# A new order for the table that drives a Mamba layer: spreads, decays, gates and one convolved pair

## The chip, the core and the metric

The kernel runs on one core of a Trainium2 chip. The metric is the device time of one execution, in microseconds (us). A core has five engines that run side by side, each in its own program order, and that wait for each other through semaphores: TensorE (PE in the profile; its weight loads are PEld), VectorE (DVE), ScalarE (ACT), GpSimd (POOL), and SyncE (SP), which here only issues DMA transfers. Below, "SP's queue" is that list of transfers: it is issued in order, and a transfer that has to wait for something holds all that stand behind it.

## What is computed

The input is 4 batches of 256 tokens of 512 channels, all in float32. There are two layers. Layer 0 is a normalisation, an attention with latent queries and keys, and a gated feed-forward network (it is the same before and after the change). Layer 1 adds two branches to x: a Mamba mixer and a feed-forward network in which a router picks two of eight low-rank experts for each token. Cut to what matters here:

```python
xn = layernorm(x)
xz = xn @ in_proj_w                         # 512 -> 2 * 1024, split in x and z
xc = silu(conv_b + causal_conv4(x))         # 4 taps, each of 1024 channels on its own
dt_r, Bm, Cm = rmsnorm of (xc @ x_proj_w)   # 32, 16 and 16 columns
dt = softplus(dt_r @ dt_proj_w + dt_bias)   # (b, 1024, 256)
for t in range(256):                        # 1024 channels x 16 states
    h = exp(dt[t] * A) * h + dt[t] * Bm[t] * xc[t]
    y[t] = sum over the 16 states of h * Cm[t]
out = x + ((y + D * xc) * silu(z)) @ out_proj_w + moe_lora(xn)
```

## The kernel before

Layer 0 ends, and layer 1's scan begins, near 327 us of the profiled execution. Layer 1's scan is cut into 128 steps u = 32 b + 4 c + g: b is the batch (0 to 3), c one of 8 blocks of 128 channels, g one of 4 groups of 4 states. In a step, 128 partitions hold 32 channels by 4 states, and the 4 x 256 free elements are the block's four parts of 32 channels by the tokens. What a step needs:

- decays u (L1087 to L1102): four Exp on ScalarE (L1099) write exp(dt * A) into one of four rotating tiles, free once scan u-4 has read its tile. The first ten steps use borrowed tiles, whose first column GpSimd clears first (L1096).
- scan_in u (L1104): an instruction of VectorE that collects the step's waits, then bx = B * (dt * x) into PSUM (L1112). It waits for decays u, for hmul u-4 and sum u-4 (below), because h has four buffers, and at g = 0 for the spread of du.
- scan u (L1116): one scan instruction over time on VectorE (L1127).
- hmul u (L1132): h * C on GpSimd. sum u (L1139, L1150): four products on TensorE that add the states up into ysum, with D * xc ahead at g = 0 (L1148).
- After the four groups of a block: take (L1156, a ScalarE copy of ysum into xc) and gate (L1161, GpSimd: xc * silu(z)).

What feeds the steps, batch by batch, is cut into small actions:

- spread n b c (L1047): four DMAs of SP's queue that bring one block's dt or du (= dt * x) from device memory, 32 channels to all 128 partitions, into one of two buffers. dt and du get to memory through step_out (GpSimd, L1020, L1022, L1024, then a send on SP's queue, L1045) and step_x (GpSimd, L1037, then a send) for a pair of blocks.
- load_x, load_z: 512 KB of projection weights for a pair of blocks on SP's queue (L625), into one of three buffers. load_late: the weights of the router and of the output (L1463). store_x: 256 KB of x to the output (L1289), to which add_to (GpSimd, L1301) adds the branches later.
- px_mm and pz_mm (L792, L1064): the projections, on TensorE. conv_in (L798 to L831): ScalarE copies px into a padded tile and makes diagonal matrices of the taps. conv_taps (L833): four products with these matrices on TensorE for the first block of a pair (L847); for its second block either four more (if the pair is listed in `both`), or ScalarE scales the four shifted rows and GpSimd adds three of them up (L854). conv_out adds the bias, conv_silu takes the whole batch's silu.
- pp_mm, pp_square, pp_norm, step_in, step_exp: B, C and dt of a batch (L958 to L985: per block two ScalarE activations at L963 and L964, then four whole ones from L982). gate_silu: silu of z with a load of the activation table ahead and one behind (L1075).
- router, choose (15 small VectorE instructions from L1198 to L1230, one a call), expert_mid, expert_turn, dense, out_mm: the second branch and the output.

Nothing schedules this: the order of each engine is the order in which the program text issues it. The text is the table `plan`, with an entry for each step u, in up to four parts divided by "|". `play(u, 0)` runs the first part before bx u, `play(u, 1)` the second between bx u and scan u, the third and fourth after scan u and hmul u:

```python
    for u in range(total + 2):
        play(u, 0)
        if u < total:
            if u:
                scan_in(u)
            play(u, 1)
            scan(u, 1 if u < total - 1 else 4)
        ...
        play(u, 2)
        play(u, 3)
```

So "decays 12" in the first part of step 9 puts four Exp at that place of ScalarE's program, and "spread dt 0 3" four transfers at that place of SP's. "rest i" are the last pieces of layer 0's feed-forward network (two products of TensorE into po each, L470), "add_last" adds them to x on VectorE (L482), "open" frees layer 0's memory. Small PSUM tiles (px, pz, pt, pdt, pp, po) share three buffers.

Of the kernel before, what the change touches and what calls it, by code (L numbers as in the profile page):

```python
# [41 lines left out]
def block_kernel(  # L42
# [614 lines left out]
    def mark(*k):  # L657
        done.add(k)
# [137 lines left out]
    both = ((1, 0), (1, 3), (2, 2), (3, 1), (3, 3),)  # L796
# [614 lines left out]
    dt = dts[0, 0]  # L1411
# [47 lines left out]
    def load_late(n, k=0, of=1):  # L1459
# [4 lines left out]
        if k == of - 1:  # L1464
# [11 lines left out]
            "decays 5, one_out 3, norm_root 1 |  | decays 4, send_dt, step_x 0 1, "  # L1476
            "add_last 5 | sum 1, rest 23, rest 24, rest 25, rest 26, rest 27, rest 28, rest 29"
        ),
        3: "spread dt 0 2 | norm_stats 2 |  | sum 2, rest 30, rest 31, rest 32, rest 33, rest 34, rest 35",
        4: "norm_scale 1 |  | add_last 6, add_last 7 | sum 3, open",  # L1480
        5: (
            "take 0 0, decays 6, decays 8, pz_mm 0 0 0, norm_turn 1 0, decays 7, norm_turn 1 1, "
            "spread du 0 2, load_z 0 1 |  | norm_copy 1 0, norm_copy 1 1 | sum 4"
        ),
        6: "decays 9, load_x 1 0, pz_mm 0 0 1, step_in 0 1 0, step_in 0 1 1, load_x 1 1 |  |  | sum 5",
        7: (
            "px_mm 1 0 0, store_x 2, load_x 1 3, gate_silu 0 0, decays 10, "
            "spread dt 0 3 |  | store_x 3, gate 0 0 | sum 6"
        ),
        8: "px_mm 1 0 1, pz_mm 0 1 0, pz_mm 0 1 1, store_x 0, store_x 1, step_exp 0 1 |  |  | sum 7",  # L1490
        9: (
            "decays 12, take 0 1, load_late rl, step_out 0 1 0 0, conv_in 1 0, px_mm 1 1 0, "
            "load_x 1 2, spread du 0 3 |  |  | sum 8"
        ),
        10: "step_out 0 1 0 1, decays 11, store_x 4, store_x 5, decays 13, conv_taps 1 0, px_mm 1 1 1",
        11: (
            "decays 14, load_z 0 2, step_out 0 1 0 2, step_x 0 2, conv_in 1 1, spread dt 0 4, "
            "px_mm 1 2 0 |  | gate 0 1 | sum 9, sum 10"
        ),
        12: "decays 15, gate_silu 0 1, conv_taps 1 1, px_mm 1 2 1 |  |  | sum 11",  # L1500
        13: "take 0 2, decays 16, step_out 0 1 1 0, spread du 0 4, conv_in 1 2, px_mm 1 3 0 |  |  | sum 12",
        14: "decays 17, conv_taps 1 2, px_mm 1 3 1",
        15: "decays 18, step_out 0 1 1 1, conv_in 1 3, spread dt 0 5 |  | load_late lb | sum 13, sum 14",
        16: (
            "decays 19, step_out 0 1 1 2, load_late bw 1 4, conv_taps 1 3, "
            "spread du 0 5 |  |  | sum 15, pz_mm 0 2 0, load_late ow 0 8"
        ),
        17: (
            "step_x 0 3, take 0 3, conv_out 1 3, decays 20, load_z 0 3, pz_mm 0 2 1, "
            "conv_silu 1 0 2 |  | gate 0 3 | sum 16, gate 0 2"  # L1510
        ),
        18: "decays 21, load_late bw 0 4 |  |  | sum 17",
        19: "decays 22, pp_mm 1 0, spread dt 0 6 |  |  | sum 18",
        20: "decays 23, load_late ow 1 8, pp_mm 1 1, spread du 0 6 |  | load_late bw 2 4 | sum 19",
        21: "take 0 4, decays 24, load_late bw 3 4, pp_square 1, load_late ow 2 8 |  | gate 0 4 | sum 20",
        22: "decays 25, pz_mm 0 3 0, load_late ow 3 8 |  | pp_norm 1, step_in 1 0 0 | sum 21",
        23: (
            "decays 26, step_exp 1 0 0, step_in 1 0 1, load_z 1 0, c_send 1, load_late ow 5 8, "
            "step_exp 1 0 1 |  | spread dt 0 7 | sum 22"
        ),  # L1520
        24: "decays 27, load_z 1 1, router 0 0, pz_mm 0 3 1, load_late ow 6 8 |  |  | sum 23",
        25: (
            "take 0 5, load_late ow 4 8, decays 28, spread du 0 7, router 0 1, gate_silu 0 3, "
            "step_out 1 0 0 0, router 0 2 |  |  | sum 24"
        ),
# [24 lines left out]
        35: "decays 38, norm_turn 2 0, dense 0 1 1 | choose | choose, add_to 0 | sum 34",  # L1550
# [289 lines left out]
```

## Time and profile before

| | us |
|---|---|
| median of 3 runs | 833.2 (830.65 to 836.03) |
| the profiled execution, its own time | 832.04 |
| its span in the trace | 829.9 |
| bx 1 starts | 330.54 |
| bx 127 starts | 817.85 |

How to read the profile: the page lists the busy time of each engine and its share of the span, then groups of instructions by line and engine ("out<-in" by the program's names), with their count, busy time, mean duration of one, idle time of the engine just before them and what ended most of it. The trace can also be asked for the waits of an engine, and for a timeline of a stretch, where a number in brackets is the idle time ahead of an instruction and what ended it. "x4" merges like instructions that follow each other. The table of stages, from the trace:

```profile
326.88:380.91 54.03, 48.44 (x238) 32.55 (x237) 41.94 (x30) 42.32 (x96) 37.60 (x31) 0.94 0.57 159
380.91:446.20 65.29, 52.41 (x302) 34.57 (x301) 60.10 (x35) 58.46 (x132) 53.21 (x34) 0.90 0.67 175
446.20:498.40 52.20, 43.84 (x226) 23.29 (x228) 51.77 (x42) 44.07 (x100) 45.10 (x27) 0.84 0.46 123
498.40:654.60 156.20, 134.29 (x734) 78.67 (x726) 153.11 (x93) 132.00 (x307) 146.69 (x94) 0.94 0.57 143
654.60:744.10 89.50, 78.18 (x394) 38.49 (x395) 86.30 (x64) 67.83 (x149) 79.29 (x49) 0.89 0.45 112
744.10:817.85 73.75, 60.13 (x286) 25.57 (x285) 66.86 (x40) 43.22 (x96) 56.68 (x33) 0.95 0.42 91
```

The columns are the stretch (start and end, us), its length, the busy time (and number of instructions) of PE, PEld, DVE, ACT and POOL, the clock that TensorE was granted, the share of the DMA engines that was busy, and GB/s. The stretches run from bx to bx: 0 to 11, 11 to 28, 28 to 41, 41 to 84, then to just before 108, and to 127.

### The profile page before, as it was taken

To read this page: it belongs to the slowest core of one execution; us is meant where nothing else is said; L and a number is where in the kernel's file an instruction comes from. 1 tells how busy PE (TensorE), PEld (TensorE's weight loads), DVE (VectorE), ACT (ScalarE), POOL (GpSimd) and SP (SyncE) were. 2 spreads that over 40 slices of the span, in tenths; PEclk is the share of its full clock that TensorE was granted. 3 is DMA by queue.
4 is the path that set the end of the run, shared out by engine and by line. 5 is a ranking of instruction groups with operands and counts; after the bars stand their busy time and mean duration, and the time that the engine had idled before them with its cause. 6 is when DMAs were issued, how large, how long until landed. Compare 5 with 4: busy or idle time off the path is not lost.

```text
span 829.9 us, 11205 instructions
## 1 busy us (share of the span) xinstructions
PE 733.8 (88%) x3802; PEld 427.4 (52%) x3802; DVE 653.5 (79%) x589; ACT 553.2 (67%) x1126; POOL 511.5 (62%) x413
## 2 busy tenths in 40 slices
PE   4999999999999999988887879797997779897984
PEld 2665545666555676666544446443465445333431
DVE  4486756287644535896899999999999899988996
ACT  4335564434556367689978887889898797826760
POOL 3133232001333432767889889979799889896875
PEclk9799999999999999999998789799899889999997
DMA  7233332001222332266595527644756453364620
GB/s 228 64 102 95 110 93 72 1 1 39 77 77 77 119 58 64 80 178 200 116 287 139 159 59 184 151 128 102 178 130 163 89 128 103 101 142 125 115 50 26
DMA packets 72194, 91.48 MB, mean 110 GB/s; under 512 B 12653, under 2 KB 54185, under 8 KB 72010
## 3 DMA queue, kind: packets, MB, share of 16 engines
q1 hardware_dynamic: 60618, 67.44, 30.6%
q0 software_dynamic: 10800, 21.50, 10.8%
q10 hardware_dynamic: 720, 1.84, 0.7%
q8 instruction: 30, 0.49, 0.2%
q14 instruction: 26, 0.21, 0.1%
HBM read 68.15 MB, written 13.42 MB: 98 GB/s over the span
## 4 chain that ended last, share of the span: by engine, by line
PE 46%; ACT 17%; DVE 17%; POOL 8%; DMA 5%; issue 5%; SPq 1%; POOLq 0%; ACTq 0%; DVEq 0%
DVE h L1127 7%; ACT decay L1099 7%; PE pg L445 6%; PE pu L445 5%; POOL h L1132 5%; DVE bx L1112 5%; PE av L398 4%; PE po L470 3%; DMA dts<-dtd 3%; PE po L1276 3%; PE px L792 3%; PE scT L387 2%; DVE mpl L355 2%; PE ysum L1150 2%; PE px L847 2%
## 5 line engine op out<-in xcount | busy, mean ns | idle before, releaser
L1132 POOL TENSOR_TENSOR h<-h,cr 128x1024 f32<-128x1024 f32 (+1 forms) x129 | 301.8, 2352 | 60.1 <-DVE h L1127 47.4
L1127 DVE TENSOR_TENSOR_SCAN h<-decay,bx 128x1024 f32<-128x1024 f32 (+1 forms) x125 | 279.0, 2234 | 4.2
L1099 ACT ACTIVATE decay<-dts,aneg 128x255 f32<-128x255 f32 x492 | 205.7, 500 | 38.6 <-DMA dts<-dtd 16.1
L1112 DVE TENSOR_TENSOR bx<-brow,dus 128x1024 f32<-128x1024 f32 x128 | 157.6, 1231 | 23.7 <-ACT decay L1099 12.8
L1150 PE MATMUL ysum<-h,stack 128*32 128x256 f32 x1016 | 85.7, 417 | 28.8 <-POOL h L1132 28.8
L457 POOL TENSOR_TENSOR hlo<-g,hhi 128x512 fp32r<-128x512 f32 x28 | 35.9, 1280 | 114.6 <-ACT hhi L456 114.6
L355 DVE TENSOR_REDUCE mpl<-sc 128x4 f32<-128x1024 f32 x64 | 76.7, 1219 | 22.7 <-PE sc L353 21.2
L428 POOL DMA_DIRECT2D wgu<-in_wgu x56 | 31.0, 555 | 95.4 <-PE pg L445 94.3
L389 ACT ACTIVATE pe<-scT 128x1024 f32<-128x1024 f32 x64 | 64.0, 1023 | 22.9 <-PE sc L353 14.3
L1325 PE MATMUL po<-ow,xc 128*128 128x512 f32 x128 | 66.5, 640 | 0.4 <-DVE xc L1733 0.4
L1150 PEld LDWEIGHTS ysum<-h,stack 128*32 128x32 f32 x1016 | 21.9, 112 | 86.1 <-POOL h L1132 49.8
L792 PE MATMUL px<-xn1T,w_in 128*128 128x256 f32 x256 | 63.2, 398 | 1.5 <-ACT dt L964 1.0
L1064 PE MATMUL pz<-xn1T,w_in 128*128 128x256 f32 x256 | 62.8, 393 | 0.0
L792 PEld LDWEIGHTS px<-xn1T,w_in 128*128 128x128 f32 x256 | 49.8, 198 | 13.9 <-issue 2.4
L1064 PEld LDWEIGHTS pz<-xn1T,w_in 128*128 128x128 f32 x256 | 48.1, 194 | 16.2 <-issue 8.9
L453 DVE SCALAR_TENSOR_TENSOR g<-g,pg 128x512 f32<-128x512 f32 x28 | 19.2, 687 | 43.0 <-ACT g L452 43.0
L445 PE MATMUL pg<-xhi,wgu 128*128 128x512 f32 x112 | 49.7, 443 | 1.2 <-ACT xhi L245 1.2
L470 PE MATMUL po<-wd,hhi 128*128 128x512 f32 x112 | 49.8, 444 | 0.0
L445 PE MATMUL pu<-xhi,wgu 128*128 128x512 f32 x112 | 47.6, 425 | 0.8 <-DVE g L455 0.8
L456 ACT CAST hhi<-g 128x512 fp32r<-128x512 f32 x28 | 17.3, 620 | 45.8 <-DVE g L455 45.8
L445 PE MATMUL pg<-xlo,wgu 128*128 128x512 f32 x112 | 44.9, 401 | 0.7 <-DVE xlo L252 0.7
L445 PE MATMUL pu<-xlo,wgu 128*128 128x512 f32 x112 | 44.3, 396 | 0.0
(243 smaller groups left out, 1306.4 us busy)
## 6 DMA issues: line engine op xcount, KB each, us to landing
dts<-dtd SPq DMA_DIRECT2D x124, 128.0 KB, 3.5
dus<-dud SPq DMA_DIRECT2D x124, 128.0 KB, 3.4
wgu<-in_wgu POOLq DMA_DIRECT2D x56, 256.0 KB, 2.7
w_in<-in_inz SPq DMA_DIRECT2D x16, 512.0 KB, 5.5
w_in<-in_inx SPq DMA_DIRECT2D x14, 512.0 KB, 5.4
dtd<-dt SPq DMA_DIRECT2D x15, 256.0 KB, 2.1
dud<-du SPq DMA_DIRECT2D x15, 256.0 KB, 2.4
wd<-in_wd POOLq DMA_DIRECT2D x7, 512.0 KB, 3.7
```

The source lines that it names most:

```text
L355: nc.vector.tensor_reduce(mpl2[b % 2][:, qb, 2 * hp : 2 * hp + 2, 16 + 2 * gq : 18 + 2 * gq], sc.rearrange("p i (f k) -> p i f k", f=2), A ...
L389: nc.scalar.activation(pes[b, k][:, 2 * t : 2 * t + 2, :], sc, AF.Exp)
L445: mm(ps, lhsT=wgus[i][:, hc, :], rhs=xs[j][:, hc, :], start=(hc == 0 and j == 0), stop=(hc == HC - 1 and j == 1))
L470: mm(po, lhsT=hids[th][j][:, m, i * P : (i + 1) * P], rhs=wd[:, m, :], start=False, stop=(m == MC - 1 and j == 1))
L792: mm(px[:, i, :], lhsT=w[:, i, hc, :], rhs=xns[b][:, hc, :], start=(hc == 0), stop=(hc == HC - 1))
L1064: mm(pz[:, i, :], lhsT=w[:, i, hc, :], rhs=xns[b][:, hc, :], start=(hc == 0), stop=(hc == HC - 1))
L1099: made["da", u] = nc.scalar.activation(da[:, k, 1:], live["dts", b, c][:, k, 1:], AF.Exp, scale=aneg[:, c, k, g : g + 1])
L1112: nc.vector.tensor_tensor(bx, brow[g // 2][:, g % 2, :].unsqueeze(1).to_broadcast([P, NG, S]), live["dus", b, c], ALU.mult)
L1127: nc.vector.tensor_tensor_scan(h[:, n].rearrange("p n t -> p (n t)"), da[:, n].rearrange("p n t -> p (n t)"), bx[:, n].rearrange("p n t -> ...
L1132: made["hc", u] = (nc.vector if k == NG - 1 else nc.gpsimd).tensor_tensor(h[:, n], h[:, n], crows[b][:, g, :].unsqueeze(1).to_broadcast([P ...
L1150: made["sum", u] = mm(ysum[k * NB : (k + 1) * NB, :], lhsT=stack, rhs=hc[:, k, :], start=False, stop=(g == NU - 1))
L1325: mm(live["po", b, i], lhsT=xcs[b][:, c, i * P : (i + 1) * P], rhs=late_w["ow"][:, c, :], start=first, stop=last)
```

## The change

The diff has three parts. In `both` the pair (3, 3) is dropped: the second block of the last pair of batch 3 is convolved by ScalarE and GpSimd instead of TensorE. In the last step a line `need("sums", total - 1)` is added, which only states what must have been issued and issues nothing. All the rest is the table: the same actions (each issued once, as before) in another order, in nearly every step from 2 to 127. Spreads are issued in front of stores and late weights; decays, step_out, gates and products of TensorE stand elsewhere. Cut to the steps that the prediction speaks of most (the others are changed in the same manner):

```diff
-    both = ((1, 0), (1, 3), (2, 2), (3, 1), (3, 3),)
+    both = ((1, 0), (1, 3), (2, 2), (3, 1),)
...
-2: (
-    "decays 5, one_out 3, norm_root 1 |  | decays 4, send_dt, step_x 0 1, "
-    "add_last 5 | sum 1, rest 23, rest 24, rest 25, rest 26, rest 27, rest 28, rest 29"
-),
-3: "spread dt 0 2 | norm_stats 2 |  | sum 2, rest 30, rest 31, rest 32, rest 33, rest 34, rest 35",
-4: "norm_scale 1 |  | add_last 6, add_last 7 | sum 3, open",
-5: (
-    "take 0 0, decays 6, decays 8, pz_mm 0 0 0, norm_turn 1 0, decays 7, norm_turn 1 1, "
-    "spread du 0 2, load_z 0 1 |  | norm_copy 1 0, norm_copy 1 1 | sum 4"
-),
-6: "decays 9, load_x 1 0, pz_mm 0 0 1, step_in 0 1 0, step_in 0 1 1, load_x 1 1 |  |  | sum 5",
-7: (
-    "px_mm 1 0 0, store_x 2, load_x 1 3, gate_silu 0 0, decays 10, "
-    "spread dt 0 3 |  | store_x 3, gate 0 0 | sum 6"
-),
-8: "px_mm 1 0 1, pz_mm 0 1 0, pz_mm 0 1 1, store_x 0, store_x 1, step_exp 0 1 |  |  | sum 7",
-9: (
-    "decays 12, take 0 1, load_late rl, step_out 0 1 0 0, conv_in 1 0, px_mm 1 1 0, "
-    "load_x 1 2, spread du 0 3 |  |  | sum 8"
-),
-10: "step_out 0 1 0 1, decays 11, store_x 4, store_x 5, decays 13, conv_taps 1 0, px_mm 1 1 1",
-11: (
-    "decays 14, load_z 0 2, step_out 0 1 0 2, step_x 0 2, conv_in 1 1, spread dt 0 4, "
-    "px_mm 1 2 0 |  | gate 0 1 | sum 9, sum 10"
-),
-12: "decays 15, gate_silu 0 1, conv_taps 1 1, px_mm 1 2 1 |  |  | sum 11",
+2: (
+    "decays 5, one_out 3, norm_root 1 |  | send_dt, step_x 0 1, add_last 5 | sum 1, rest 23, "
+    "decays 4, rest 24, rest 25, rest 26, rest 27, rest 28, rest 29, rest 30, rest 31, "
+    "rest 32, rest 33, rest 34, rest 35"
+),
+3: "spread dt 0 2 | norm_stats 2",
+4: "norm_scale 1 |  | add_last 6, add_last 7 | sum 2, sum 3, open",
+5: (
+    "take 0 0, decays 6, pz_mm 0 0 0, norm_turn 1 0, norm_turn 1 1, spread du 0 2, "
+    "load_z 0 1 |  | norm_copy 1 0, norm_copy 1 1 | sum 4"
+),
+6: (
+    "decays 9, load_x 1 0, decays 8, decays 7, spread dt 0 3, pz_mm 0 0 1, store_x 1, "
+    "step_in 0 1 0, step_in 0 1 1, load_x 1 1, gate_silu 0 0 |  |  | sum 5"
+),
+7: "px_mm 1 0 0, load_x 1 3, decays 10 |  | gate 0 0 | sum 6",
+8: "px_mm 1 0 1, pz_mm 0 1 0, pz_mm 0 1 1, step_exp 0 1 |  |  | sum 7",
+9: (
+    "decays 12, take 0 1, px_mm 1 1 0, step_out 0 1 0 0, store_x 5, conv_in 1 0, "
+    "load_late rl, store_x 2, load_x 1 2 |  | gate 0 1 | sum 8"
+),
+10: (
+    "step_out 0 1 0 1, decays 11, store_x 4, decays 13, conv_taps 1 0, px_mm 1 1 1, "
+    "step_out 0 1 1 0 |  | spread du 0 3, step_out 0 1 1 1 | store_x 3"
+),
+11: (
+    "decays 14, load_z 0 2, step_out 0 1 0 2, step_x 0 2, conv_in 1 1, spread dt 0 4, "
+    "px_mm 1 2 0, gate_silu 0 1 |  |  | sum 9, sum 10"
+),
+12: "decays 15, conv_taps 1 1 |  |  | sum 11",
...
-13: "take 0 2, decays 16, step_out 0 1 1 0, spread du 0 4, conv_in 1 2, px_mm 1 3 0 |  |  | sum 12",
-14: "decays 17, conv_taps 1 2, px_mm 1 3 1",
-15: "decays 18, step_out 0 1 1 1, conv_in 1 3, spread dt 0 5 |  | load_late lb | sum 13, sum 14",
-16: (
-    "decays 19, step_out 0 1 1 2, load_late bw 1 4, conv_taps 1 3, "
-    "spread du 0 5 |  |  | sum 15, pz_mm 0 2 0, load_late ow 0 8"
-),
-17: (
-    "step_x 0 3, take 0 3, conv_out 1 3, decays 20, load_z 0 3, pz_mm 0 2 1, "
-    "conv_silu 1 0 2 |  | gate 0 3 | sum 16, gate 0 2"
-),
+13: "take 0 2, px_mm 1 2 1, spread du 0 4, conv_in 1 2, px_mm 1 3 0, step_out 0 1 1 2 |  |  | sum 12",
+14: "decays 16, conv_taps 1 2, decays 17, store_x 0, px_mm 1 3 1, conv_in 1 3",
+15: "decays 18, spread dt 0 5 |  | load_late lb | spread du 0 5, sum 13, sum 14",
+16: "decays 19, conv_taps 1 3 |  | decays 20 | pz_mm 0 2 0, sum 15",
+17: (
+    "step_x 0 3, take 0 3, conv_out 1 3, pz_mm 0 2 1, load_z 0 3, conv_silu 1 0 2, "
+    "load_late bw 1 4 |  |  | sum 16, load_late ow 0 8"
+),
...
-22: "decays 25, pz_mm 0 3 0, load_late ow 3 8 |  | pp_norm 1, step_in 1 0 0 | sum 21",
-23: (
-    "decays 26, step_exp 1 0 0, step_in 1 0 1, load_z 1 0, c_send 1, load_late ow 5 8, "
-    "step_exp 1 0 1 |  | spread dt 0 7 | sum 22"
-),
-24: "decays 27, load_z 1 1, router 0 0, pz_mm 0 3 1, load_late ow 6 8 |  |  | sum 23",
+22: (
+    "decays 25, spread du 0 6, load_z 1 0, load_late ow 1 8 |  | pp_norm 1, step_in 1 0 0, "
+    "gate 0 4 | sum 21"
+),
+23: (
+    "decays 26, step_exp 1 0 0, pz_mm 0 3 0, step_in 1 0 1, c_send 1, step_exp 1 0 1, "
+    "load_late bw 3 4, load_late ow 2 8 |  |  | sum 22"
+),
+24: (
+    "pz_mm 0 3 1, decays 27, router 0 0, load_late ow 3 8, "
+    "load_late ow 5 8 |  | spread dt 0 7 | sum 23"
+),
...
-31: "spread dt 1 1 | choose | choose, decays 34 | sum 30",
-32: (
-    "decays 35, spread du 1 1, step_out 1 0 1 2, b_rows 1 1, gate_silu 1 0 1, norm_root 2, "
-    "load_x 2 0 | choose | choose | sum 31"
-),
-33: (
-    "take 0 7, decays 36, gate 0 7, step_x 1 1, step_in 1 1 0, "
-    "dense 0 0 0 | choose | choose | sum 32"
-),
+31: "spread dt 1 1, pz_mm 1 1 1 |  | choose, decays 34",
+32: (
+    "spread du 1 1, step_out 1 0 1 2, sum 30, load_x 2 1, norm_root 2, load_x 2 0, "
+    "gate_silu 1 0 1, step_x 1 1 | choose, choose | b_rows 1 1, decays 35, choose | sum 31"
+),
+33: "take 0 7, dense 0 0 0, decays 36, step_in 1 1 0 | choose | choose | sum 32",
...
-36: (
-    "decays 39, spread du 1 2, step_out 1 1 0 0, norm_copy 2 0, norm_turn 2 1, "
-    "load_x 2 2 | choose | choose | sum 35"
-),
+36: (
+    "decays 39, step_out 1 1 0 0, norm_copy 2 0, norm_turn 2 1, "
+    "step_out 1 1 1 0 | choose | choose | sum 35"
+),
...
-41: "take 1 1, step_out 1 1 1 0, conv_taps 2 0, px_mm 2 1 1, px_mm 2 2 0 |  |  | sum 40",
-42: "decays 45, spread dt 1 4, decays 44, conv_in 2 1, px_mm 2 3 0 |  | gate 1 1 | sum 41",
+41: "take 1 1, conv_taps 2 0, px_mm 2 1 1, px_mm 2 2 1 |  |  | sum 40",
+42: "decays 45, load_z 1 3, conv_in 2 1, decays 44, px_mm 2 3 0 |  |  | sum 41",
...
-75: "px_mm 3 3 0, decays 78 |  | gate 2 1 | sum 74",
-76: "decays 79, spread du 2 4, load_z 2 3, conv_in 3 2, step_out 2 1 1 2 |  |  | sum 75",
-77: "take 2 2, step_x 2 3, decays 80, conv_taps 3 2, px_mm 3 3 1 |  |  | sum 76",
+75: "decays 78, step_out 2 1 1 0, step_out 2 1 1 1, step_out 2 1 1 2, conv_taps 3 1 |  |  | sum 74",
+76: "decays 79, spread du 2 4, load_z 2 3, px_mm 3 2 1, conv_in 3 2, px_mm 3 3 0 |  |  | sum 75",
+77: "take 2 2, gate 2 1, decays 80, conv_taps 3 2 |  |  | sum 76",
...
-80: "spread du 2 5, decays 83, pz_mm 2 2 1, conv_taps 3 3, conv_out 3 3 |  | gate 2 2 | sum 79",
+80: "decays 83, pz_mm 2 2 1, spread du 2 5, conv_taps 3 3, conv_out 3 3 |  |  | sum 79",
...
-104: (
-    "decays 107, out_mm 1 1 4, out_mm 1 1 5, out_mm 1 1 6, step_out 3 1 1 0, step_x 3 2, "
-    "spread du 3 3, load_z 3 2, spread dt 3 3 |  |  | sum 103"
-),
-105: "take 3 1, decays 108, out_mm 1 1 7 |  | gate 3 1, expert_mid 2 0 | sum 104",
-106: (
-    "decays 109, spread dt 3 4, out_mm 2 0 0, out_mm 2 0 1, step_out 3 1 1 1, "
-    "load_z 3 3 |  |  | sum 105"
-),
-107: "decays 110, step_out 3 1 1 2, out_mm 2 0 2, out_mm 2 0 3, out_mm 2 0 4, expert_turn 2",
+104: (
+    "decays 107, out_mm 1 1 4, out_mm 1 1 5, out_mm 1 1 6, step_out 3 1 1 0, spread du 3 3, "
+    "load_z 3 2, step_out 3 1 1 1, spread dt 3 3, out_mm 1 1 7 |  | expert_mid 2 0, "
+    "spread dt 3 4 | sum 103"
+),
+105: "take 3 1, decays 108, out_mm 2 0 0 |  |  | sum 104",
+106: "step_x 3 2, decays 109, out_mm 2 0 1, load_z 3 3 |  |  | sum 105",
+107: "out_mm 2 0 2, out_mm 2 0 3 |  |  | step_out 3 1 1 2",
...
+            need("sums", total - 1)
```

## The prediction

> **What bounds the kernel now.** I read the page first (busy shares, groups), then the starts of the VectorE instructions from 326 us on, then the table of VectorE's waits for that stretch, and last the timelines of ScalarE and of SP's queue around the longest two.
>
> ```profile
> PE 733.8 (88%) x3802; PEld 427.4 (52%) x3802; DVE 653.5 (79%) x589; ACT 553.2 (67%) x1126; POOL 511.5 (62%) x413
> ...
> L1132 POOL TENSOR_TENSOR h<-h,cr 128x1024 f32<-128x1024 f32 (+1 forms) x129 | 301.8, 2352 | 60.1 <-DVE h L1127 47.4
> L1127 DVE TENSOR_TENSOR_SCAN h<-decay,bx 128x1024 f32<-128x1024 f32 (+1 forms) x125 | 279.0, 2234 | 4.2
> L1099 ACT ACTIVATE decay<-dts,aneg 128x255 f32<-128x255 f32 x492 | 205.7, 500 | 38.6 <-DMA dts<-dtd 16.1
> L1112 DVE TENSOR_TENSOR bx<-brow,dus 128x1024 f32<-128x1024 f32 x128 | 157.6, 1231 | 23.7 <-ACT decay L1099 12.8
> ```
>
> TensorE has the highest share, but that is an average over two layers. Layer 1 is the 128 steps from bx 0 (326.88) to bx 127 (817.85), and in most of them VectorE runs without a hole: a bx (1.23 us), a scan (2.29) and two gaps of 0.035, 3.587 us a step. At that rhythm 127 steps would take 455.5 us; they took 491.0. The 35 us between are waits, VectorE's own other instructions and slow first steps:
>
> ```profile
> DVE bx L1112 <- ACT decay L1099: 12.8, 2, 8.3
> DVE bx L1112 <- PE ysum L1150: 5.5, 4, 2.1
> DVE x L482 <- PE po L470: 2.2, 1, 2.2
> ```
>
> (Columns: us in total, times, the longest.) A new order removes no step, so all it can win is in these lines and in VectorE's small instructions. By place, from the starts of bx: bx 11 waits 8.33 us, bx 17 1.83, bx 20 0.61, bx 27 1.37, bx 28 0.40, bx 85 2.14, bx 108 4.49, bx 110 1.11: 20.3 us. The two longest:
>
> ```profile
> 374.41 1.70 ACT L1099 ACTIVATE decay<-dts,aneg 128x255 f32<-128x255 f32 x4 [2.80 <-DMA dts<-dtd]
> 376.02 0.35 ACT L1156 COPY xc<-ysum 128x256 f32<-128x256 f32 x1
> 376.27 0.58 ACT L810 COPY pad<-px 128x512 f32<-128x512 f32 x1
> 376.75 1.28 ACT L815 ACTIVATE dg<-cst,vec 128x128 f32<-128x128 f32 x4
> 377.93 1.27 ACT L820 ACTIVATE tap<-cst,vec 128x128 f32<-128x128 f32 x4
> 379.10 3.29 ACT L1099 ACTIVATE decay<-dts,aneg 128x255 f32<-128x255 f32 x8
> ```
> ```profile
> 746.79 1.70 ACT L1099 ACTIVATE decay<-dts,aneg 128x255 f32<-128x255 f32 x4 [8.29 <-DMA dts<-dtd]
> ```
> ```profile
> 731.37 0.38 SPq L1045 DMA_DIRECT2D dtd<-dt  x1
> 736.13 0.38 SPq L1045 DMA_DIRECT2D dud<-du  x1
> 736.62 1.83 SPq L1053 DMA_DIRECT2D dus<-dud  x4
> 738.89 0.36 SPq L625 DMA_DIRECT2D w_in<-in_inz  x1
> 739.34 2.75 SPq L1053 DMA_DIRECT2D dts<-dtd  x6
> ```
>
> bx 11 comes after decays 11 (first half of the last row of the first fence, to 380.80), which stand behind conv_in 1 0, a take and decays 12; only the 2.80 us ahead of decays 12 are a transfer. bx 108 is a transfer alone: SP stood from 731.8 to 736.1 for du of pair 2 (step_x 3 2 on GpSimd), and the spread of dt 3 3 queued behind it.
>
> **The change part by part.** Each term is against the profiled execution, 832.04 us with a span of 829.9.
>
> Steps 2 to 11. (a) The rests of layer 0 run together with no sum between: one sum of 0.64 us less ahead of add_last 7, for which VectorE waited 2.2 us (L482); 0.65 earlier. (b) Decays 9 now stand in front of 8 and 7. They need GpSimd's memset (L1096), behind hmul 5, which ended at 356.79, now about 356.15. Decays 9, 8, 7 at 1.70 each end at 361.2, while scan 7 started at 359.38: about 1.9 us lost. (c) ScalarE is then busy without a hole: step_in (8 rows from 359.28 to 362.27, 2.9) to 364.1, gate_silu (3.2, from 362.29 to 365.5) to 367.3, decays 10 and step_exp (365.50 to 371.62, 6.1) to 373.4, decays 12 (1.7) to 375.1. No transfer is waited for: spread dt 0 3, issued at 367.26 behind load_x 1 3, now goes before it. take, conv_in and decays 11 as before, 374.41+1.61 to 380.80, 4.8: 379.9. So bx 11 starts near 380.0, **0.9 won**; (a) and (b) vanish in what is left of its wait, and 6 of its 8 us stay, because ScalarE's queue is full where before it stood for a DMA.
>
> bx 17 waited for sum 13, on TensorE behind a conv_taps (3.55 us) and a px_mm (1.89). The taps of pair 3 and its px now come after or a step earlier, the sum ends between 399.9 and 401.7 and bx 17 is due at 401.6: **1.6 won** of 1.83 (bounds 0 and 1.83). bx 20: send dt and its spread go earlier, **0.6**. bx 21: decays 21 follow conv_silu in step 17 and no decays 20 stand between: **0.4 lost**. bx 27 and 28: step_in 1 0 1 waited behind pz on TensorE; pz_mm 0 3 0 is now behind step_exp, and decays 27 end about 437.6 where bx 27 is due about 438.5: **1.8 won** (1.37+0.40).
>
> choose, steps 30 to 39, are VectorE instructions:
>
> ```profile
> L1221 DVE TENSOR_TENSOR sel<-sel,b 128x32 f32<-128x32 f32 x1 | 1.4, 1394 | 0.0
> ...
> L1206 DVE TENSOR_TENSOR sel<-sel,m 128x32 f32<-128x32 f32 x1 | 0.2, 195 | 0.0
> ```
>
> The same operation takes 0.2 or 1.4 us: those between a bx and its scan end when GpSimd's hmul ends, those just behind a scan find GpSimd between two instructions. Four two-input ones stood in front of a scan (L1200, L1209, L1217, L1221), four do so after (L1202, L1209, L1217, L1221). GpSimd has more behind it there (step_x 1 1 a step earlier, step_out 1 1 1 0 four): **0.5 lost**, bounds 1.2 won (one such less) and 5.9 lost (below). The Trainium skill, GPSIMD Engine Reference, section Key points, says that GpSimd shares its SBUF interfaces with VectorE and contends with instructions of two SBUF inputs; the rows agree (1.4 us against 0.2). By that rule alone each two-input choose is at risk, wherever GpSimd is late.
>
> Step 42: decays 44 behind conv_in 2 1 (3.5 us of ScalarE): **0.6 lost**, between 0 and 1. Steps 45 to 84: decays end 2 us or more ahead of their bx, so I cost the moves at nothing. The cover is that slack and GpSimd's: from 498.4 to 654.6 it was busy 146.69 of 156.2 us, and pair (3,3) adds three additions (L854, 0.73 each, 2.4 with gaps). By its order it runs up to 4 us later around steps 75 to 80, and hmul 80 ends about 652.4, bx 84 at 654.59 needs it.
>
> bx 85 waited for sum 81 behind pp_mm 3 0, which waited for conv_silu (655.40, idle 3.54). One convolved channel less takes 4 products (1.9 us) from TensorE in front of the conv_out that conv_silu waits for, and four scalings (1.28) from ScalarE against four activations (0.55 + 3 x 0.5): silu about 2 us sooner, **1.9 won** (bounds 0 and 2.14; the additions, ending near 650.0, come before silu by 1.3). bx 93: decays 93 behind step_exp moved forward, **0.3 lost**. The second choose, steps 92 to 102, stands in the same places: nothing, within 0.5.
>
> bx 108: step_x 3 2 and its send move from step 104 behind both spreads to 106. SP, free at 731.8, then issues spread du 3 3, load_z and spread dt 3 3 in the rhythm it had from 736.6: dt about 734.4 instead of 739.34, five us earlier. Decays 108, which ended at 748.5, end near 743.5, and bx 108 is due at 744.15: **4.5 won**, with 0.7 to spare (bounds 0 and 4.49). bx 110: the sum finds TensorE free, **1.1 won**. Steps 111 to 127: decays, sums and spreads keep at least a step ahead; nothing. The tail of 12 us from bx 127 is untouched.
>
> Sum: won 0.9 + 1.6 + 0.6 + 1.8 + 1.9 + 4.5 + 1.1 = 12.4; lost 0.4 + 0.5 + 0.6 + 0.3 = 1.8; net 10.6. From 832.04 that is 821.4; the median is 1.2 above the profiled run, so **822.6 us** on the scale of 833.2.
>
> **The rivals.**
> 1. *New waits give most of it back.* Nearly every step has another order; I followed each by durations of the old rows, and those cannot settle where a margin is 0.7 to 1.5 us (bx 17, 84, 91, 108). For it: bx 17 to bx 28 hang on TensorE, whose clock was 0.90 there and 0.84 behind. Also here: all nine two-input chooses at the long price, 5 more at 1.19 = 5.9. Net gain 1 to 7 us: 826 to 832, middle 828.5. By the page named above this is what a later GpSimd does.
> 2. *The SP change doesn't do what it says:* spread dt 3 3 also waits for something else, its buffer (decays 103) or an earlier landing, so bx 108 keeps its 4.5 and bx 110 its 1.1: 828.2. Against: it was issued 0.45 us after the load in front of it, with no pause of its own.
> 3. *Slower: GpSimd becomes the bound* from step 45 to 84. It needs 146.7 + 2.4 = 149.1 of 156.2 us, 95%. Decisive point: an hmul more than 8.4 us late (bx u waits for hmul u-4: four steps are 14.35 us, and an hmul ends 5.9 after its bx at the earliest), or 4.8% more GpSimd time per step. Beyond that each percent costs 1.5 us, and 10.6 us, the forecast's gain, are gone at 12%: 833 and up; 842 at 18%. For it: 94% busy; against: its rows have one duration, 2.35.
> 4. *More is won:* ScalarE reaches decays 9 without a wait and bx 11 gains 3 us more, choose 1.2: 818.
>
> **How the numbers follow.** Forecast 0.50 (its own range 818 to 826), rival 1 0.20, rival 2 0.08, rival 3 0.14, rival 4 0.08. About 1%, 8.3 us, is what a measurement of this kernel can tell from no change; faster by that is below 824.9, slower above 841.5. The forecast puts three quarters of itself and rival 4 all below 824.9: 0.46. Rivals 1 and 2, a quarter of the forecast and a quarter of rival 3 are within: 0.44. Slower 0.10. The range 815 to 836 leaves out the far half of rival 3 and a little of rival 4.
>
> **What would show it.** Right: bx 108 and bx 110 follow at 3.59 us, with no idle time at decays 108; bx 85's wait under 0.5; bx 17, 20, 27, 28 without wait; bx 11 still waiting 5 to 7 us for ScalarE with no transfer ahead of decays 12; scan 7 waiting about 1.9 for decays 7. Wrong: a wait over 1 us between steps 41 and 84 or behind 111, choose instructions of 1.4 us more than four times, an hmul as the releaser of a bx.

## The result and the profile after

The changed kernel took 822.72 us (median of 4 runs, 822.27 to 826.75) beside 831.95 for the kernel before (4 runs, 830.65 to 836.03): a ratio of 0.989, 95% interval 0.9859 to 0.9921, so 0.8 to 1.4% faster. The forecast was 822.6. The total came out as forecast, but not all of its terms did: two of them were wrong by 2.6 and 5.1 us, in opposite directions. The profiled execution took 822.62 us, with a span of 820.5.

The first view is the page after: busy shares, and the groups of hmul, scan, decays and bx.

```profile
PE 728.6 (89%) x3794; PEld 425.0 (52%) x3794; DVE 657.9 (80%) x589; ACT 553.9 (68%) x1125; POOL 513.8 (63%) x416
...
L1132 POOL TENSOR_TENSOR h<-h,cr 128x1024 f32<-128x1024 f32 (+1 forms) x129 | 303.0, 2356 | 52.9 <-DVE h L1127 33.8
L1127 DVE TENSOR_TENSOR_SCAN h<-decay,bx 128x1024 f32<-128x1024 f32 (+1 forms) x125 | 279.0, 2234 | 4.6 <-ACT decay L1099 0.5
L1099 ACT ACTIVATE decay<-dts,aneg 128x255 f32<-128x255 f32 x492 | 205.5, 499 | 35.1 <-DVE h L1127 18.6
L1112 DVE TENSOR_TENSOR bx<-brow,dus 128x1024 f32<-128x1024 f32 x128 | 157.6, 1231 | 9.2 <-PE px L847 5.3
```

The line to look at is the last. All 128 bx waited 23.7 us before and 9.2 now, 14.5 less; yet the span is only 9.4 shorter. VectorE's busy time tells where most of the rest is: 657.9 against 653.5, 4.4 us more, with the same 589 instructions. A wait inside an instruction counts as busy, as the instruction shown below tells (4.19 us for 0.17). The waits of VectorE for layer 1 (columns as before: us in total, times, the longest):

```profile
DVE bx L1112 <- PE px L847: 5.3, 1, 5.3
DVE x L1332 <- PE po L1325: 1.9, 1, 1.9
DVE x L482 <- PE po L470: 1.4, 1, 1.4
DVE xc L1739 <- PE ysum L1150: 1.3, 1, 1.3
DVE b L1219 <- ACT e L1212: 1.3, 1, 1.3
DVE nrm L904 <- ACT rs L725: 1.0, 1, 1.0
DVE h L1127 <- ACT decay L1099: 0.5, 1, 0.5
```

Of the waits of a bx the one of bx 11 is left (5.3; the release put down to PE px is inferred: decays 11 ended 0.2 us before it, and nothing of bx 11 hangs on px), and 0.35 at bx 27. Three waits are new: L1219, a choose; L904, pp_norm 2; and 0.5 ahead of scan 7, for its decays. And of the 4.4 us of busy time 4.0 stand in one instruction. VectorE's timeline behind step 98:

```profile
702.79 1.23 DVE L1112 TENSOR_TENSOR bx<-brow,dus 128x1024 f32<-128x1024 f32 x1
705.32 0.19 DVE L1219 TENSOR_REDUCE b<-sel 128x4 f32<-128x32 f32 x1 [1.30 <-ACT e L1212]
...
711.20 4.19 DVE L1225 TENSOR_TENSOR sel<-sel,e 128x32 f32<-128x32 f32 x1
715.32 1.22 DVE L1112 TENSOR_TENSOR bx<-brow,dus 128x1024 f32<-128x1024 f32 x1
```

In the kernel before, the same instruction:

```profile
718.67 0.17 DVE L1225 TENSOR_TENSOR sel<-sel,e 128x32 f32<-128x32 f32 x1
```

GpSimd's timeline of the changed kernel at that time:

```profile
707.84 2.37 POOL L1132 TENSOR_TENSOR h<-h,cr 128x1024 f32<-128x1024 f32 x1 [1.32 <-DVE sel L1221]
710.15 0.88 POOL L1301 DMA_DIRECT2D out<-x  x1
710.76 1.03 POOL L1161 TENSOR_TENSOR xc<-xc,sz 128x256 f32<-128x256 f32 x1
711.45 2.65 POOL L1132 TENSOR_TENSOR h<-h,cr 128x1024 f32<-128x1024 f32 x1
713.76 1.57 POOL L1020 TENSOR_TENSOR e<-u,e 128x512 f32<-128x512 f32 x1
715.41 1.27 POOL L1022 TENSOR_TENSOR e<-e,lw 128x512 f32<-128x512 f32 x1
```

Add starts and durations: the DMA of add_to 4 ends at 711.03, but the gate behind it starts at 710.76; the gate ends at 711.79 and hmul 100 starts at 711.45; it ends at 714.10 and step_out starts at 713.76. Each starts 0.3 us before the one ahead has ended and is recorded 0.3 longer than usual (1.03 for 0.73, 2.65 for 2.36, 1.57 for 1.27). VectorE's choose ended only at 715.39, in the first gap (715.33 to 715.41).

Where the time went, by the start of bx (a minus is earlier than in the kernel before; forecast in the same sign):

| place | measured | forecast |
|---|---|---|
| before bx 0 (layer 0, not changed) | -1.1 | 0 |
| bx 1 to 11 | -3.5 | -0.9 |
| bx 17, 20, 21 | -2.4 | -1.8 |
| bx 27, 28 | -1.4 | -1.8 |
| first choose, to bx 41 | +0.2 | +0.5 |
| bx 44 | 0 | +0.6 |
| bx 54 (pp_norm 2) | +1.1 | 0 |
| bx 64 (L754 beside a step_x) | +0.3 | 0 |
| bx 85 | -2.1 | -1.9 |
| bx 93 | 0 | +0.3 |
| second choose, to bx 104 | +5.1 | 0 |
| bx 108, bx 110 | -5.5 | -5.6 |
| bx 127 | -9.3 | -10.6 |

The largest gain beyond the forecast is in bx 1 to 11. ScalarE and GpSimd of the changed kernel where the prediction had decays 9, 8 and 7 wait for a memset:

```profile
352.85 4.89 ACT L1099 ACTIVATE decay<-dts,aneg 128x255 f32<-128x255 f32 x12 [0.18 <-DMA dts<-dtd]
```
```profile
354.78 0.11 POOL L1096 MEMSET decay<- 128x4 f32 x1
```

The 1.1 us ahead of bx 0 come from no part of the change: among the profiled executions of all kernels below, whose layer 0 is the same, bx 0 starts between 325.3 and 327.6.

### The profile page after: what moved, and what is told of

Read it like the earlier page. It is cut to its first block, busy times and chain, and to the rows that moved or that the text cites. A ratio compares the mean times of both kernels' runs of the same rounds, so it can differ in the third digit from the quotient of the medians.

```text
span 820.5 us, 11182 instructions
## 1 busy us (share of the span) xinstructions
PE 728.6 (89%) x3794; PEld 425.0 (52%) x3794; DVE 657.9 (80%) x589; ACT 553.9 (68%) x1125; POOL 513.8 (63%) x416
## 4 chain that ended last, share of the span: by engine, by line
PE 39%; DVE 32%; POOL 11%; ACT 7%; issue 7%; DMA 3%; SPq 1%; ACTq 0%; POOLq 0%; DVEq 0%
DVE h L1127 16%; DVE bx L1112 10%; POOL h L1132 7%; PE pg L445 7%; PE pu L445 5%; PE av L398 4%; PE po L470 4%; ACT decay L1099 3%; PE scT L387 2%; DVE mpl L355 2%; PE po L1276 2%; PE px L792 2%; PE ysum L1150 1%; PE po L465 1%; PE sc L353 1%
## 5 line engine op out<-in xcount | busy, mean ns | idle before, releaser
L792 PE MATMUL px<-xn1T,w_in 128*128 128x256 f32 x256 | 66.1, 412 | 5.2 <-ACT xn1T L780 3.1
L792 PEld LDWEIGHTS px<-xn1T,w_in 128*128 128x128 f32 x256 | 51.5, 206 | 18.9 <-ACT xn1T L780 4.2
```

Source lines behind the costliest of these rows:

```text
L792: mm(px[:, i, :], lhsT=w[:, i, hc, :], rhs=xns[b][:, hc, :], start=(hc == 0), stop=(hc == HC - 1))
```

## The experiments

Theory at the start: from step 28 on VectorE is the bound, so every wait of VectorE that goes or comes counts in full; in steps 5 to 28 it is ScalarE. And L1225 was held by GpSimd. Kernels that start from the kernel before are marked so; the others start from the changed one.

**e1, both actions out of step 99.**

```diff
-98: "spread du 3 1, decays 101, step_in 3 1 1 |  | choose | sum 97",
-99: "... | choose | add_to 4, choose, gate 2 7",
-101: "... |  | choose"
+98: "spread du 3 1, decays 101, step_in 3 1 1 |  | gate 2 7, choose | sum 97",
+99: "... | choose | choose",
+101: "... |  | add_to 4, choose",
```

> The changed kernel with two actions put back where they stood before: gate 2 7 in step 98, add_to 4 in step 101 (step 99 holds only its choose). Theory GpSimd: choose's L1225 in step 100 took 4.19 us because gate 2 7 and add_to 4 left GpSimd without a pause from 710.15 to 715.33; expected: L1225 0.2 us, bx 101 4.0 us earlier, 1.0 more of it lost or won at L1219 at most, time 822.7 - 4.0 = 818.7. Rival ScalarE: L1225 waits for e of L1212 or for what is queued behind it; expected: 4.2 us as before, time 822.7.

Measured: 819.76 us (4 runs, 818.54 to 820.77), ratio 0.9851 (0.981 to 0.9892) to the kernel before. VectorE's timeline of e1, the same instruction:

```profile
710.91 0.17 DVE L1225 TENSOR_TENSOR sel<-sel,e 128x32 f32<-128x32 f32 x1
711.03 1.23 DVE L1112 TENSOR_TENSOR bx<-brow,dus 128x1024 f32<-128x1024 f32 x1
```

0.17 for 4.19, bx 101 4.00 us earlier by its own step, and nothing after it changes. The rival with ScalarE is out.

**e2 and e3, one of the two actions alone.** e2 moves add_to 4 only, e3 gate 2 7 only, with the lines of e1.

> The changed kernel with add_to 4 alone put back in step 101; gate 2 7 stays in step 99. Theory overlap: behind a DMA of GpSimd the next instructions start 0.3 us before the one ahead has ended, so that VectorE's two-input instruction finds no gap between them; without the DMA it waits for one instruction at most: L1225 0.2 to 0.9 us, time 819 to 820. Rival work: it is the amount of GpSimd's work in a row that counts, DMA or not: L1225 2.5 to 4 us, time 821.5 to 822.7.

> The changed kernel with gate 2 7 alone put back in step 98; add_to 4 stays in step 99. Both GpSimd theories: hmul 100 cannot start before scan 100 has ended, nothing else stands behind the DMA, so L1225 finds GpSimd idle: 0.2 us, time 818.7. If the DMA itself holds VectorE back, L1225 takes 0.5 us or more; if neither counts, 4.2 us.

Measured: e2 820.89 us (one run), L1225 0.17; e3 817.14 (one run), L1225 0.17. Either move is enough. (Of the 3.7 us between the two runs 1.5 stand ahead of bx 0, and 1.2 in the second choose, where L1219 did not wait in e3.) But they don't tell the two theories of GpSimd apart: in e2 the gate ran from 712.09 to 712.82 and was over when choose came (at 713.1), and in e3 GpSimd had a gap of 0.6 us there. The row that the rival "work" needs was not met. For this there is e9.

**e9, the same row without a DMA.**

```diff
-99: "spread dt 3 2, step_x 3 1, decays 102, step_exp 3 1 | choose | add_to 4, choose, gate 2 7",
+99: "spread dt 3 2, decays 102, step_exp 3 1 | choose | choose, step_x 3 1, gate 2 7",
-101: "... |  | choose"
+101: "... |  | add_to 4, choose",
```

> The changed kernel with add_to 4 put back in step 101 and step_x 3 1 (1.27 us of GpSimd, no DMA) put in its place in step 99, ahead of gate 2 7: GpSimd works without a pause through hmul 99, step_x, gate, hmul 100 and step_out, as in the changed kernel, but with no DMA in the row. Theory overlap (instructions start 0.3 us before the one ahead has ended only behind a DMA of GpSimd, and that is what shuts VectorE out): L1225 in step 100 gets in behind the instruction that runs when it comes, 0.2 to 1.0 us. Theory work (any row without a pause shuts it out): L1225 3 to 4.3 us.

Measured: 819.56 us (one run). GpSimd's timeline of e9, and VectorE's:

```profile
707.94 2.36 POOL L1132 TENSOR_TENSOR h<-h,cr 128x1024 f32<-128x1024 f32 x1 [2.57 <-DVE sel L1221]
710.26 1.28 POOL L1037 TENSOR_TENSOR du<-dt,xc 128x512 f32<-128x512 f32 x1
711.49 0.73 POOL L1161 TENSOR_TENSOR xc<-xc,sz 128x256 f32<-128x256 f32 x1
712.18 2.36 POOL L1132 TENSOR_TENSOR h<-h,cr 128x1024 f32<-128x1024 f32 x1
714.50 1.27 POOL L1020 TENSOR_TENSOR e<-u,e 128x512 f32<-128x512 f32 x1
```
```profile
711.27 0.31 DVE L1225 TENSOR_TENSOR sel<-sel,e 128x32 f32<-128x32 f32 x1
```

GpSimd works without a pause from 707.94 to 715.77, but now each instruction starts only 0.04 us before the one ahead ends, with its usual duration. L1225 came while step_x ran, waited for its end (711.54) and was done at 711.58, while the gate ran from 711.49 to 712.22 and did not hold it. So it is not the amount of work: it is the row behind a DMA.

**e10, the row put into the kernel before.** Starts from the kernel before.

```diff
-98: "... |  | gate 2 7, choose | sum 97",
-99: "... | choose | choose",
-101: "... |  | gate 3 0, add_to 4, choose | sum 100"
+98: "... |  | choose | sum 97",
+99: "... | choose | add_to 4, choose, gate 2 7",
+101: "... |  | gate 3 0, choose | sum 100",
```

> The kernel before with gate 2 7 (from step 98) and add_to 4 (from step 101) moved to step 99 as the change does, add_to ahead of choose, nothing else. If the row of DMA, gate, hmul 100 and step_out on GpSimd is the cause, L1225 in step 100, 0.17 us before, takes 2.5 to 4.3 us here too: time 832 + 2.5 to 4 = 834.5 to 836. If something else of the changed kernel is needed, 0.2 us and 832.

Measured: 839.86 us (one run). GpSimd and VectorE of e10:

```profile
722.27 0.87 POOL L1301 DMA_DIRECT2D out<-x  x1
722.88 1.03 POOL L1161 TENSOR_TENSOR xc<-xc,sz 128x256 f32<-128x256 f32 x1
723.58 2.64 POOL L1132 TENSOR_TENSOR h<-h,cr 128x1024 f32<-128x1024 f32 x1
725.90 1.54 POOL L1020 TENSOR_TENSOR e<-u,e 128x512 f32<-128x512 f32 x1
```
```profile
723.33 4.17 DVE L1225 TENSOR_TENSOR sel<-sel,e 128x32 f32<-128x32 f32 x1
```

The same row, the same overlaps, and 4.17 us for 0.17. The step cost 3.97 us by bx 101. e5 and e6 below leave step 99 as the change has it, and their L1225 took 4.18 us each. (The run is 8 us above the median of the kernel before and above the expected 834.5 to 836; the rest are waits in steps 5 to 28, which differ from run to run: bx 11, 17, 23 and 27 together waited 5.8 us longer than in the profile ahead of the prediction, and bx 0 came 1.6 earlier.)

**e4, the SP part of step 104 alone.** Starts from the kernel before.

```diff
-104: "..., step_out 3 1 1 0, step_x 3 2, spread du 3 3, load_z 3 2, spread dt 3 3 |  |  | sum 103"
-106: "decays 109, spread dt 3 4, ..."
+104: "..., step_out 3 1 1 0, spread du 3 3, load_z 3 2, spread dt 3 3 |  |  | sum 103",
+106: "step_x 3 2, decays 109, spread dt 3 4, ...",
```

> The kernel before with one action moved: step_x 3 2 (and its send of du on SP's queue) from step 104, ahead of the spreads of block 3 of batch 3, to step 106. Theory SP: SP stood 4.4 us for that send, so spread dt 3 3 is issued about 734.5 instead of 739.34 and bx 108 loses its wait of 4.49; bx 110 may keep its 1.11. Expected 832.0 - 4.5 = 827.5. Rival: the spread waits for something else or the transfer takes longer, bx 108 still waits 2 us or more: 830 to 832.

Measured: 825.72 us (10 runs, 822.38 to 828.09), ratio 0.9919 (0.9894 to 0.9944). SP's queue and VectorE of e4:

```profile
733.40 1.86 SPq L1053 DMA_DIRECT2D dus<-dud  x4
735.36 0.37 SPq L625 DMA_DIRECT2D w_in<-in_inz  x1
736.16 1.74 SPq L1053 DMA_DIRECT2D dts<-dtd  x4
```
```profile
743.40 2.29 DVE L1127 TENSOR_TENSOR_SCAN h<-decay,bx 128x1024 f32<-128x1024 f32 x1
745.72 1.23 DVE L1112 TENSOR_TENSOR bx<-brow,dus 128x1024 f32<-128x1024 f32 x1
```

The pause of SP is gone; bx 108 (745.72) follows scan 107 (to 745.69) without a wait, 4.46 us won, and bx 110 wins its 1.08 with it. One action moved by two steps makes 5.5 of the 9.3 us.

**e7, the convolved pair alone.** Starts from the kernel before; `both` without (3, 3).

> The kernel before with pair (3, 3) dropped from both, nothing else. Prediction's theory: silu of batch 3 comes 2 us sooner, pp_mm 3 0 ends before sum 81 is due, bx 85 loses its 2.14 us (0 to 0.3 left), hmul 80 to 84 cost nothing: time 832 - 2 = 830. Rival: silu waits for GpSimd's three additions, which stand behind hmul 79 or 80: bx 85 still waits 1 us or more, 831 to 833.

Measured: 831.18 us (one run). In its trace bx 85 follows bx 84 after 3.59 us (654.97, 658.56): the 2.14 are gone, 2.10 won at this place, as in the changed kernel. The time of the one run can't show it, since other waits differ both ways from the profile ahead of the prediction (bx 11 and 17 2.6 us less; bx 20, 27, 78 and 110 3.3 more).

**e8, the spread in front of the load alone.** Starts from the kernel before.

```diff
-6: "decays 9, load_x 1 0, pz_mm 0 0 1, ..."
-7: "px_mm 1 0 0, store_x 2, load_x 1 3, gate_silu 0 0, decays 10, spread dt 0 3 | ..."
+6: "decays 9, load_x 1 0, spread dt 0 3, pz_mm 0 0 1, ...",
+7: "px_mm 1 0 0, store_x 2, load_x 1 3, gate_silu 0 0, decays 10 | ...",
```

> The kernel before with spread dt 0 3 moved from step 7 (behind load_x 1 3) to step 6 (behind load_x 1 0). Theory: of bx 11's 8.3 us, the transfer ahead of decays 12 makes 2.8, the rest is ScalarE's order: bx 11 waits 5.5 us, time 832 - 2.8 = 829. Rival: the load issued behind the spread then lands late and px_mm 1 1 or step_in waits, bx 11 or bx 17 lose 1 us or more: 830 to 832.

Measured: 826.96 us (one run). VectorE of e8 at bx 11:

```profile
376.08 1.23 DVE L1112 TENSOR_TENSOR bx<-brow,dus 128x1024 f32<-128x1024 f32 x1 [4.91 <-ACT decay L1099]
```

The wait falls from 8.33 to 4.91, 3.4 us, about what all of the change won in bx 1 to 11 (3.5). The size is less sure than that: with these steps left as they were, bx 11 waited 7.6 us in e7, 9.5 in e10 and 10.2 in e4. Of the 5.0 us in the time, 1.4 stand ahead of bx 0.

**e5, decays 11 early.**

```diff
-8: "px_mm 1 0 1, pz_mm 0 1 0, pz_mm 0 1 1, step_exp 0 1 |  |  | sum 7",
-10: "step_out 0 1 0 1, decays 11, store_x 4, decays 13, ...
+8: "decays 11, px_mm 1 0 1, pz_mm 0 1 0, pz_mm 0 1 1, step_exp 0 1 |  |  | sum 7",
+10: "step_out 0 1 0 1, store_x 4, decays 13, ...
```

> The changed kernel with decays 11 moved from step 10 (behind conv_in 1 0) to the front of step 8 (behind decays 10). Theory ScalarE: bx 11 waits 5.3 us for ScalarE's program order alone (decays 10, step_exp, decays 12, take, conv_in, decays 11 without a pause); decays 11 now end about 367, decays 12 about 373.2 (bx 12 due 374.6), decays 13 about 377.9 (bx 13 due 378.2): the 5.3 us go, time 822.7 - 5 = 817.5, less what bx 17, 21 or 27 then wait. Rival: what follows is no earlier than before (taps, px and step_in of batch 1 on TensorE and ScalarE), so that bx 12 to bx 28 wait for it instead: 820.5 to 822.7.

Measured: 825.96 us (4 runs, 824.42 to 826.57), ratio 0.9923 (0.9896 to 0.995): 3.2 more than the changed kernel's 822.72. The two intervals overlap; by the starts of bx, in one execution of each, e5 is 3.4 us later at bx 127. VectorE's waits of e5 from 326 to 450 us:

```profile
DVE bx L1112 <- PE px L847: 2.6, 1, 2.6
DVE bx L1112 <- ACT decay L1099: 2.1, 2, 1.4
DVE bx L1112 <- ACT dg L815: 1.8, 1, 1.8
DVE bx L1112 <- PE ysum L1150: 1.6, 1, 1.6
```

bx 11 no longer waits, but bx 12 waits 2.6 us (to 377.27; the last quarter of spread du 0 3, which landed at 377.1 in e5 and at 377.4 in the changed kernel, where bx 12 came at 379.9), bx 13 1.8 (sum 9 on TensorE, behind conv_taps and px_mm), bx 16 1.4, bx 19 1.6, bx 21 and 27 together 1.3 more than in the changed kernel. The rival holds, and more: step_exp, take and conv_in moved back by 1.6 us, what stands behind decays 13 by 0.8. The table of stages for 352 to 416 us, first the kernel before, then the changed one, then e5 (columns as in the table of stages ahead of the prediction):

```profile
352.00:416.00 64.00, 54.27 (x296) 38.15 (x295) 51.98 (x30) 57.81 (x127) 48.13 (x33) 0.92 0.63 170
```
```profile
352.00:416.00 64.00, 53.84 (x313) 36.19 (x311) 56.87 (x34) 63.27 (x142) 54.45 (x36) 0.97 0.73 204
```

```profile
352.00:416.00 64.00, 54.59 (x312) 37.57 (x310) 54.21 (x32) 60.06 (x133) 53.61 (x35) 0.95 0.70 196
```

ScalarE was busy 57.8 of the 64 us before, 63.3 in the changed kernel and 60.1 in e5. So in the changed kernel it has next to no room in this stretch, and what one bx gains by a new order among its instructions others lose. That ScalarE alone bounds the stretch is not shown: the wait of bx 12 is for a transfer, that of bx 13 for TensorE.

**e6, the first choose laid out as the second.** The two-input chooses (L1202, L1209, L1217, L1221) stand behind a scan, add_to 0 goes to step 41.

```diff
-32: "... | choose, choose | b_rows 1 1, decays 35, choose | sum 31"
-35: "... | choose | add_to 0, choose | sum 34"
-36: "... | choose | choose | sum 35"
-37: "... |  | choose, load_x 2 3",
-38: "... |  | gate 1 0, choose | sum 36, sum 37",
+32: "... |  | choose, b_rows 1 1, decays 35 | sum 31",
+35: "... | choose | choose | sum 34",
+36: "... |  | choose | sum 35",
+37: "... | choose | choose, load_x 2 3",
+38: "... | choose | choose, gate 1 0 | sum 36, sum 37",
...
+40: "... |  | choose | sum 39",
+41: "... |  | add_to 0 | sum 40",
```

> The changed kernel with the first choose (steps 30 to 39) laid out as the second one is: the two-input instructions behind a scan, single-input ones in front of one; add_to 0 moved from step 35 to 41, gate 1 0 behind its choose. Theory GpSimd's port: four two-input ones (L1202, L1209, L1217, L1221) took 1.29 to 1.39 us between a bx and its scan, since hmul ran; behind a scan they take 0.2 to 0.9, about 0.9 us less each; time 822.7 - 3.3 = 819.4. Rival: GpSimd is as busy behind the scans in these steps (step_out, step_x, gates), the waits only move: 821.5 to 824.

Measured: 820.04 us (4 runs, 818.12 to 821.74), ratio 0.9847 (0.9815 to 0.9879). The longest and the shortest of the four in e6 (count, busy us, mean ns of one), from 450 to 490 us:

```profile
L1217 DVE TENSOR_TENSOR sel<-sel,cst 128x32 f32<-128x32 f32 x1 | 0.3, 302 | 0.0
...
L1221 DVE TENSOR_TENSOR sel<-sel,b 128x32 f32<-128x32 f32 x1 | 0.2, 165 | 0.0
```

From 1.29 to 1.39 us each to 0.17 to 0.30 (L1202 185 ns, L1209 168): 4.6 us won by bx 37. But 0.4 came back at once (L1219 waits for ScalarE's e), and 2.3 at one place:

```profile
500.52 1.23 DVE L1112 TENSOR_TENSOR bx<-brow,dus 128x1024 f32<-128x1024 f32 x1 [2.32 <-ACT decay L1099]
```

This is bx 44: decays 44 stand behind conv_in 2 1, as the prediction feared for the changed kernel itself; there the margin just held, and here VectorE comes earlier.

**e11 and e12, the found losses mended.** On e6's order: decays 44 and 45 change places around conv_in 2 1; pp_norm 2 and step_in 2 0 0 go from step 53 to 54; gate 2 7 to step 98, add_to 4 to step 105. e11 has the last six of the second choose one place later, so that L1219 does not wait; e12 has the tenth and eleventh both behind scan 99 and the rest as in the change.

> The changed kernel with its found losses mended together: both chooses with their two-input instructions behind a scan, add_to 0, add_to 4 and gate 2 7 out of their way, the last six of the second choose one place later so that L1219 (1.3 us behind ScalarE's e) does not wait, pp_norm 2 one step later (1.0 us at L904), decays 44 ahead of conv_in 2 1 and decays 45 behind it (2.3 us at bx 44 when the first choose is shorter). Theory: VectorE is the bound from step 28 on, so the terms add: 4.0 + 4.2 + 1.1 + 1.2 = 10.5, time 822.7 - 10.5 = 812.2. Rival: ScalarE or GpSimd stands behind as it does in steps 5 to 28, waits come back at other bx: 815 to 820.

> The kernel of e11 with the second choose laid out once more: its tenth and eleventh both behind scan 99, the rest where the change has them (in e11 they were one place later each, where L1227 took 1.69 and L1230 0.85 us because GpSimd's step_out and gate were running). Theory: L1219 still does not wait for ScalarE's e, L1225, L1227 and L1230 take 0.2 us: bx 104 2.1 us earlier than in e11, time 815.1 - 2.1 = 813. Rival: the eleventh, with two inputs and now second behind the scan, meets hmul 99 and takes 1.3 us or more: 814 to 815.

Measured: e11 815.07 us (6 runs, 813.0 to 817.37), ratio 0.9797 (0.9756 to 0.9837); e12 814.62 (6 runs, 812.34 to 817.04), ratio 0.9777 (0.9747 to 0.9806), 2.2% faster than the kernel before (1.9 to 2.5). By the starts of bx, e11 is 8.0 us ahead of the changed kernel at bx 127, not 10.5: in the second choose L1227 waited for an hmul that two step_out had held up (1.69 us) and L1230 for a step_out (0.85), and the first choose won 3.5 where 4.2 were expected. In e12 L1221, second behind scan 99, took 0.80 behind a step_x, L1219 of this choose waits no more, and bx 127 comes 1.9 us earlier than in e11; the medians (0.45 apart) are too close to show that, by their intervals.

## Why the prediction was right

Forecast 822.6, measured 822.7. The mechanism of most terms was right; that the total came out so close is luck, as the last paragraph shows.

- bx 108 and 110: forecast 4.5 and 1.1, measured 4.5 and 1.1, and shown alone (e4). SP had stood for one send. Spread dt 3 3 was issued from 730.1 on, and decays 108 had margin.
- bx 85: forecast 1.9, measured 2.1, shown alone (e7). GpSimd's additions did no harm, and rival 3 fell: from bx 41 to bx 84 it was busy 146.2 of 158.0 us, and no bx waited for an hmul.
- bx 17, 20, 27, 28: forecast 4.0 together, measured 3.8. What won the 1.8 us of bx 17 is not shown. With the order of the kernel before, bx 17 waited 1.8 us in its own profile, 2.7 in e4 and e10, 0.9 in e8, and none in e7. In the four that waited, TensorE's granted clock from bx 14 to bx 17 was 0.85 to 0.87, and the eight products of conv_taps 1 2 (L847) took 3.3 to 3.7 us; in e7 the clock was 1.00 and they took 2.00. So the wait went with the clock. In all nine executions with the changed order the clock was 1.00 there, and no run tells what that order would do at the lower one.
- These sizes are those of one execution of the kernel before. In others that left the steps concerned as they were, bx 108 waited 3.4 to 5.4 us (e7, e8, e10) and bx 85 1.5 to 2.1 (e4, e8, e10). A forecast that a wait goes to nothing meets its size exactly when both are read from the same profile.
- Step (b), "They need GpSimd's memset (L1096), behind hmul 5", was wrong. Of the three only decays 9 has a memset at L1096. In the changed kernel decays 9, 8 and 7 ran together from 352.85, and the memset only from 354.78: it clears the first column, and the Exp write the others. So decays 7 made scan 7 wait 0.5 us, not 1.9, ScalarE's row behind them started 2.5 us earlier than forecast (counted from bx 0), and bx 11, which this row bounds, came 2.6 earlier. The term was 0.9 and measured 3.5. e8 shows that most of it hangs on spread dt 0 3, which I had put at 2.8 and then given back to the memset.
- "The second choose ... stands in the same places: nothing, within 0.5" was the step that failed most: +5.1 us. The places of choose were the same; I had not followed what was moved around them on GpSimd. 4.0 is the row behind add_to 4 (e1, e9, e10), 1.3 is L1219 behind ScalarE's e, and L1227 gave 0.2 back. It is also the one sign of being wrong that showed: a fifth long choose.
- pp_norm 2 stands a step earlier than before and then waits for its root on ScalarE: +1.1, not looked at (the wait itself is 1.00 us, at the bound that the prediction set for waits between steps 41 and 84). The waits forecast at bx 21, 44 and 93 (1.3 together) did not come.

The misses add up to -2.6 - 1.3 + 5.1 + 1.4 = +2.6, and with some tenths layer 1 won 8.2 us where 10.6 were forecast; the 1.1 us ahead of bx 0 and the 1.2 by which the forecast was raised from one execution to the median made up for the rest. No step of the prediction gave either: the first lies ahead of the change, and with a fourth run the median of the kernel before is 831.95, no higher than its profiled execution. The sum was closer than its terms, by luck. Rival 1 was right in part: GpSimd did make a choose long, but at the second choose, through a single instruction and through what stood in its row, not by being later. The first choose behaved as forecast (four at 1.29 to 1.39 us). The Trainium skill, GPSIMD Engine Reference, section Key points, has VectorE's instructions of two SBUF inputs contend with GpSimd; e6 (1.3 to 1.4 us against 0.2) and e1 (4.19 against 0.17) agree.

## What to carry to other kernels

Follow a moved action on every engine on which it issues, and look at what it puts around the work that stays in place: here an unmoved 0.17 us instruction became 4.2 us. Before removing a wait, look at the busy share of the engine that ends it over the stretch around: at 99% (ScalarE, 352 to 416 us) the new order of e5 moved the wait and added to it, while a wait behind an idle queue (SP in step 104) went by moving one transfer. Before crediting a won wait to the new order, look at other executions of the old one, and at the clock there: the wait of bx 17 was gone in one of them. Compare busy times too: a wait inside an instruction shows there and in no list of waits.

## What the runs showed of the hardware

Behind a DMA that GpSimd issues, its next instructions started 0.26 to 0.34 us before the one ahead had ended and were recorded 0.3 us longer, one after the other, until a pause (changed kernel 710.15 to 715.33, e10 722.27 to 727.44); in a row without a DMA the overlap was 0.04 to 0.05 us (e9). Other DMAs of add_to are followed by the same (kernel before, 726.87 to 736.10). A VectorE instruction with two SBUF inputs got in between two instructions of the latter row (0.31 us) and not between those of the former (4.17 to 4.19 us in the changed kernel, e5, e6 and e10): it waited for three of them. Where the row had no DMA, a choose of two inputs that found GpSimd at work ended 0.04 to 0.06 us behind the instruction that ran when it came (L1209 of the changed kernel at 459.72, its hmul at 459.67). That the overlap is what shuts it out is the likely reading, and GpSimd's recorded starts and ends are rough; shown is only that the row with the DMA does it and the row without it doesn't.
